# Layer 0 of a four-layer scan network as one sequence of scans

## The chip, the core and the metric

The kernel runs on one core of a Trainium2 chip. The metric is the device time of one execution in microseconds (us). Engines are called PE (matrix), DVE (vector), ACT (scalar), POOL (GpSimd) and SP (which here issues all the transfers). Everything is computed in float32.

## The reference, cut to what matters

The network has four layers over images of 4 x 48 x 48 x 192. The change concerns layer 0, two "bimambas" with a norm and a residual between them:

```python
xw = jnp.swapaxes(x, 1, 2).reshape(Bb, Ww * Hh, C)
xw = _bimamba(xw, 0, P)                      # pair 0
xh = jnp.swapaxes(xw.reshape(Bb, Ww, Hh, C), 1, 2).reshape(Bb, Hh * Ww, C)
xh = _ln(xh, norm_w, norm_b) + x.reshape(Bb, -1, C)   # the "mix"
xh = _bimamba(xh, 2, P)                      # pair 2
# _bimamba(u, i, P) = _mamba(u, P[i]) + _mamba(u[:, ::-1], P[i + 1])
```

A `_mamba` projects 192 channels to 2 x 384 (inner part and gate z), runs a causal convolution of three taps and a silu over the sequence, projects to dt, B and C, and makes for each of 384 channels and 16 states the recurrence

```python
h = exp(delta * A) * h + (delta * u) * b      # over the 2304 tokens
y = sum over the 16 states of h * c
```

then adds D * u, multiplies by silu(z) and projects back to 192. The second sequence order is the image by rows where the first was by columns, so the mix has to turn each image.

## The kernel before, in words

**A job** (`MambaJob`, L496) is 384 tokens of one image in one direction; six make a pass. Layer 0 has for each pair four images x two passes x six jobs = 48 jobs. The backward pass of an image adds the forward pass's result (`prior`) to its own, and stores it mirrored. **A group** is 128 channels x 4 states x 384 tokens; a job has 3 x 4 = 12, and its groups are called slots 0 to 11 here. One group does:

- ACT makes the four decays `a` (`decay`, L365), two groups ahead;
- DVE multiplies `du` by the broadcast B rows `bcb` into `inputs`, and scans (`scan`, L401);
- POOL copies the scan's last column into `state`, multiplies `h` in place by the C rows (`weigh`, L419), and writes the entering state of the next group but one into its `bcb` (`carry`, L382, the copy `bcb<-state`);
- PE sums the four states of `h` into `y` by identity matmuls (`reduce`, L433), one group behind; a float32 matmul is two instructions.

`h` goes round a ring of four buffers (`hs`), `bcb` one of five in layer 0 and in layer 3 (`bcs`), where a job fetches four, each 1540 KB broadcast from DRAM.

**The order** is written out by hand in `run_jobs` (L738). PE, DVE, POOL and ACT work in the order of the program; only SP's transfers are placed by the scheduler. Besides the group's own steps each slot has the *units* of the next job (`units`, L548: projections, convolution, dt, gate, each a PE part and an ACT part) and the *outputs* of the previous one (L625). A backward job's outputs end with two adds of `prior` on POOL, in slots 7 and 8. So a job's preparation runs while the job before it scans. POOL also has `drive` (slots 1, 5, 9) and `gate` (slots 2, 6, 10), each one product of 128 x 384.

`mamba_pair` (L899) loads the weights of a pair, opens the pools and runs its 48 jobs. It is called twice (L1616 to L1623). Between, `mix_images` (L926) runs by itself: it loads the sums of all images, normalizes them in stages on PE, DVE and ACT (`norm_stages`), turns them and adds the residual on DVE and POOL (L956), writes `mixed`, and loads pair 2's weights, whose diagonal matrices DVE makes (L859, L866).

Layers 1 and 2 already have **side steps**: a `Side` (L692) holds lists of small steps, and each slot may begin one whose kind (`pe`, `act`, `pool`, `both`, `dma`) is allowed in that slot. `Normed` (L1146) makes the steps of a layer norm. Layer 0 doesn't use them.

Of the kernel before, what the change touches and what calls it, by code (L numbers as in the profile page):

```python
# [17 lines left out]
B = 4  # L18
# [204 lines left out]
class ScanPools:  # L223
# [6 lines left out]
    def __init__(self, k, ctx, parts, rows):  # L230
        pool = k.tc.tile_pool
        self.parts, self.rows = parts, rows
        self.wide = 128 // parts
        self.n = N // parts
        self.groups = self.n // NG
        self.W = W = CH if rows else CH + 1
        self.one = ctx.enter_context(pool(name="one", bufs=1))
        self.two = ctx.enter_context(pool(name="two", bufs=2))
        self.bcs = ctx.enter_context(pool(name="bcs", bufs=5 if parts == 1 else 4))
        self.hs = ctx.enter_context(pool(name="hs", bufs=4))  # L240
        self.y = ctx.enter_context(pool(name="y", bufs=2 if rows else 1, space=PSUM))
        self.ps = ctx.enter_context(pool(name="ps", bufs=2, space=PSUM))
        self.vec = ctx.enter_context(pool(name="vec", bufs=1, space=PSUM))

        inputs = k.tile(self.vec, [128, 1536 if rows else 2048], "inputs")
        self.b = inputs[:, : NG * W].rearrange("p (j l) -> p j l", l=W)
        self.du = k.tile(self.vec, [128, 512], "du")[:, :W]
        self.ones = k.tile(self.one, [128, 1], "ones")
        k.nc.vector.memset(self.ones, 1.0)
        self.decays = [k.tile(self.one, [128, NG, W], f"a{i}") for i in range(3)]  # L250
        self.n_decays = 0
        self.revs = [None] * 3
        self.yts = 3 if rows else 2
        self.rev = None

        self.sum = k.ident
        if parts == 2:
            self.sum = k.tile(self.one, [128, 64], "sum")
            k.nc.vector.tensor_tensor(self.sum, k.ident[:, :64], k.ident[:, 64:], ALU.add)
# [28 lines left out]
class ScanJob:  # L288
# [6 lines left out]
    extras = ()  # L295

# [199 lines left out]
class MambaJob(ScanJob):  # L496
# [5 lines left out]
    skips = True  # L502
# [45 lines left out]
    def units(self, last):  # L548
# [41 lines left out]
        if self.twin is not None:  # L590
            self.z = self.twin.z
            outputs = last.outputs((7, 7), (9, 9), (10, 10), (11, 11)) if last is not None else []
            bc, deltas = self.projections(lambda: self.xs, (3, 3), (5, 5))
            return [conv(0, 0, 0), conv(1, 1, 2), conv(2, 2, 2), bc, *deltas, *outputs]
        outputs = last.outputs((4, 4), (6, 6), (7, 7), (8, 8)) if last is not None else []
# [29 lines left out]
    def outputs(self, *slots):  # L625
# [10 lines left out]
        def add(m):  # L636
            k.g.tensor_tensor(self.o[:, m, :], self.o[:, m, :], prior[:, m, :], ALU.add)
            if m == 1:
                store()
# [24 lines left out]
        if self.prior is not None:  # L664
            prior = k.tile(self.pools.one, [Q, 2, CH], "prior")
            k.nc.sync.dma_start(prior, halves(self.prior)[:, :, d0 : d0 + CH])
            units += [(slots[2 + m], lambda: None, lambda m=m: add(m)) for m in range(2)]
# [24 lines left out]
class Side:  # L692
# [4 lines left out]
    slots = {"pe": (0, 4, 5), "both": (0, 4), "act": (0, 4, 5), "pool": (0, 2, 4, 5), "dma": range(6)}  # L697

    def __init__(self, k, psum):
        self.k, self.psum = k, psum  # L700
        self.waiting, self.rest = [], None
# [36 lines left out]
def run_jobs(jobs, side=None):  # L738
# [29 lines left out]
    for t in range(len(groups) + gated):  # L768
# [8 lines left out]
        if at == taken + 3 and n + 1 == len(jobs) and n:  # L777
            Stream(jobs[n - 1].outputs(*[(0, 0)] * 4)).run(per)
# [20 lines left out]
        if side is not None and t < len(groups):  # L799
            if at == taken + 1 and n:  # L800
# [10 lines left out]
    Stream(jobs[-1].outputs(*[(0, 0)] * 4)).run(per)  # L811
# [37 lines left out]
class MambaWeights(Weights):  # L849
    def __init__(self, k, pool, inT, xpT, dtT, vec, tag):  # L850
        super().__init__(k, pool, 128, 12, xpT, dtT, vec, tag)
        self.decays(k)
        nc = k.nc
        self.k, self.pool, self.in_src = k, pool, inT
        self.D = self.vec[:, :, 17:18]
        self.cb = self.vec[:, :, 18:19]
        self.diagD = k.tile(pool, [128, 3, 128], f"diagD{tag}")
        for i in range(3):
            nc.vector.tensor_scalar(  # L859
                self.diagD[:, i, :], k.ident, self.D[:, i, :], None, ALU.mult  # L860
            )
        self.taps = vec.shape[1] - 19
        self.diag = k.tile(pool, [128, 3, self.taps, 128], f"diag{tag}")
        for i in range(3):
            for t in range(self.taps):
                nc.vector.tensor_scalar(  # L866
                    self.diag[:, i, t, :],
                    k.ident,
                    self.vec[:, i, 19 + t : 20 + t],
                    None,  # L870
                    ALU.mult,
                )

    def enter(self, tag="inT"):

        self.inT = self.k.tile(self.pool, [Q, 2, 768], tag)
        self.k.nc.sync.dma_start(self.inT, self.in_src.rearrange("(k p) m -> p k m", p=Q))

# [20 lines left out]
def mamba_pair(k, weights, srcs, first, outs, ahead=None):  # L899


    with ExitStack() as ctx:
        pool = ctx.enter_context(k.tc.tile_pool(name="w", bufs=1))
        ws = []

        def load():
            for n, (inT, xpT, dtT, vec, outT) in enumerate(weights):
                w = MambaWeights(k, pool, inT, xpT, dtT, vec, f"_{n}")
                w.enter(f"inT_{n}")
                w.outT = k.tile(pool, [128, 3, C], f"outT_{n}")  # L910
                k.nc.sync.dma_start(w.outT, outT.rearrange("(k p) m -> p k m", p=128))
                ws.append(w)

        if ahead is None:
            load()
        else:
            ahead(load)
        pools = ScanPools(k, ctx, 1, False)
        jobs = []
        for b in range(B):  # L920
            jobs += mamba_pass(k, pools, ws[0], False, srcs[b], first[b])
            jobs += mamba_pass(k, pools, ws[1], True, srcs[b], outs[b], True, first[b])
        run_jobs(jobs)


def mix_images(k, o, hw, norm, out_hw, load):  # L926

    nc, tc = k.nc, k.tc
    with (
        tc.tile_pool(name="mx", bufs=2) as pool,  # L930
        tc.tile_pool(name="mx1", bufs=1) as one,
        tc.tile_pool(name="mxp", bufs=6, space=PSUM) as psum,
    ):
        nw = k.tile(one, [Q, 2, 2], "nw")
        s0, s1, res = {}, {}, {}

        def fetch(b):
            s0[b] = k.tile(pool, [Q, 2, L], "s0")
            for n in range(2 if b == 0 else 1):
                at = slice(0, L) if b else (slice(0, CH), slice(CH, L))[n]  # L940
                nc.sync.dma_start(s0[b][:, :, at], halves(o[b])[:, :, at])
                if b == 0 and n == 0:
                    nc.sync.dma_start(nw, norm.rearrange("(k p) v -> p k v", p=Q))
            s1[b] = k.tile(pool, [Q, 2, L], "s1")
            res[b] = k.tile(pool, [Q, 2, L], "res")
            nc.sync.dma_start(res[b], halves(hw[b]))

        def pre(b):
            if b + 1 < B:
                fetch(b + 1)  # L950
            if b == 1:
                load()

        def post(b):
            for m in range(2):
                (nc.vector, nc.gpsimd)[m].tensor_tensor(  # L956
                    square(res[b][:, m, :]),
                    square(res[b][:, m, :]),
                    flipped(s1[b][:, m, :]),
                    ALU.add,  # L960
                )
                nc.sync.dma_start(out_hw[b][m * Q : (m + 1) * Q, :], res[b][:, m, :])

        def chunk(img):
            return lambda b, c: img[b][:, :, c * CH : (c + 1) * CH]

        stages = norm_stages(
            k, pool, psum, chunk(s0), chunk(s1), k.mean192, 1e-5, nw[:, :, 0], nw[:, :, 1]
        )
        fetch(0)  # L970
        pipelined(stages, pre, post)
# [174 lines left out]
class Normed:  # L1146
# [22 lines left out]

    def image(self, c, src, steps, dst):  # L1170

        def move(out, in_):
            return lambda: self.k.nc.sync.dma_start(out, in_)

        def parts(out, in_):
            n = L // 3
            at = [slice(i * n, (i + 1) * n) for i in range(3)]
            return [[("dma", move(out[:, :, a], in_[:, :, a])) for a in at]]  # L1180

        ahead = parts(self.turned, src) if c == NCH - 1 else []
        return [*ahead, steps, *(parts(dst, self.turned) if c == 0 else [])]
# [25 lines left out]
    def norm(self, srcs, eps, g, bias, out, tag="nx", last="act"):  # L1209
# [22 lines left out]
        def root(ps):  # L1232
            rs = st["rs"] = self.tile([Q, CH], "nrs")
            k.act(rs, ps, AF.Ln, bias=self.eps[:, eps : eps + 1])
            k.act(rs, rs, AF.Exp, scale=-0.5)
            scale(0)
# [5 lines left out]
        def affine(dst, m):  # L1242
# [7 lines left out]
            ("both", (Q, lambda: [(k.mean192, st["sq"][:, m, :]) for m in range(2)], root)),  # L1250
            ("pool", lambda: scale(1)),
# [38 lines left out]
def scan_layers(k, pool, layers, ends, ahead):  # L1290
# [4 lines left out]
    with ExitStack() as ctx:  # L1295
# [5 lines left out]
        side = Side(k, pools.ps)  # L1301
# [166 lines left out]
class RowWeights:  # L1468
# [4 lines left out]
    def __init__(self, k, pool, raw, psum, sets):  # L1473
        self.pairs = []
        for s, (ws, _) in enumerate(sets):
            w = MambaWeights(k, pool, *ws[:4], f"_{s}")
            self.pairs.append((w, copy(w)))
# [122 lines left out]
def network(tc, d, out):  # L1600
    with ExitStack() as ctx:
# [8 lines left out]
        def pair(first):  # L1610
# [5 lines left out]
        hw, wh = ([d[n][b] for b in range(B)] for n in ("x_hw", "x_wh"))  # L1616
        first, o = images("first"), images("oa")
        mamba_pair(k, pair(0), wh, first, o)
        mixed, x1 = images("mixed"), images("x1")
        mamba_pair(  # L1620
            k, pair(2), mixed, first, x1,
            lambda load: mix_images(k, o, hw, d["L0_norm"], mixed, load),
        )  # L1623
# [90 lines left out]
def layout(i):  # L1714
    x = np.moveaxis(i["x"], -1, 1)
    d = {"x_hw": x.reshape(B, C, L), "x_wh": swapped(x).reshape(B, C, L)}
# [82 lines left out]
```

## Time and profile before

| | us |
|---|---|
| median of 3 runs (19842.79 to 19854.58) | 19849.5 |
| the profiled execution | 19853.7 |
| its span | 19851.9 |
| DVE busy | 18186.9 (92%) |
| PE busy | 17508.4 (88%) |
| POOL busy | 14713.3 (74%) |
| ACT busy | 12793.6 (64%) |
| mean granted PE clock | 0.939 |

Layer 0's first pair scans from 44.8 us to 3136.5 us, its second from 3335.4 to 6426.5; then come the inputs of layer 1, the scans of layers 1 and 2, of layer 3, and the last part. The rows of the timeline read: start, duration, engine, line (often a helper's: L56 is the wrapper of DVE, POOL and PE, L93 that of ACT), operation, output<-inputs, shape, and in brackets the engine's idle time before it with what ended it. A busy PE is not PE at its peak, since matmuls overlap.

### The profile page before, as it was taken

How to read it: one execution, taken by the hardware profiler on the slowest of the kernel's cores; microseconds unless marked ns; L12 is line 12 of the kernel's file. 1: busy time of each engine (PE TensorE's matmuls, PEld its weight loads, DVE VectorE, ACT ScalarE, POOL GpSimd, SP SyncE). 2: the span in 40 equal slices, each digit the busy share in tenths (PEclk: the TensorE clock that was granted, in tenths of full speed). 3: DMA queues.
4: the chain of work that ended last, by engine and by line, in shares of the span. 5: the costliest groups of instructions: out<-in, count | busy, mean ns of one | idle time of the engine just before them, and what ended most of it. 6: DMA issues, size and time to landing. Idle time of an engine off the chain costs nothing. (4 is left out here: it accounts for less than half of the span.)

```text
span 19851.9 us, 159333 instructions
## 1 busy us (share of the span) xinstructions
PE 17508.4 (88%) x48144; PEld 8277.2 (42%) x48144; DVE 18186.9 (92%) x7432; ACT 12793.6 (64%) x22445; POOL 14713.3 (74%) x10864
## 2 busy tenths in 40 slices
PE   8999997999998878888888888889999989999989
PEld 4444443444444422333333333334444444444444
DVE  8999997999999599999999999969999999999993
ACT  6666665666666466666666766766666666666663
POOL 7887875888787177888888888857777777777770
PEclk9999998999999989999999999989999999999999
DMA  3333333333333366666666666642233233332331
GB/s 116 107 110 114 108 107 120 106 109 115 112 107 106 79 134 139 146 145 148 143 145 146 138 145 144 139 115 104 104 107 106 99 108 109 107 106 103 108 107 46
DMA packets 495754, 2313.41 MB, mean 117 GB/s; under 512 B 76360, under 2 KB 329584, under 8 KB 340336
## 3 DMA queue, kind: packets, MB, share of 16 engines
q1 hardware_dynamic: 494896, 2303.22, 41.3%
q8 instruction: 386, 6.32, 0.1%
q14 instruction: 472, 3.87, 0.1%
HBM read 2110.68 MB, written 192.32 MB: 116 GB/s over the span
## 5 line engine op out<-in xcount | busy, mean ns | idle before, releaser
L56 POOL TENSOR_TENSOR h<-h,bcb 128x1536 f32<-128x1536 f32 x3456 | 11909.0, 3446 | 1712.8 <-DVE h L56 1437.2
L56 DVE TENSOR_TENSOR_SCAN h<-a,inputs 128x1540 f32<-128x1540 f32 (+1 forms) x3456 | 11609.1, 3359 | 449.8 <-ACT a L93 12.0
L93 ACT ACTIVATE a<-delta,A 128x384 f32<-128x384 f32 (+1 forms) x13824 | 7432.7, 602 | 3325.5 <-DVE h L56 3312.8
L56 PE MATMUL y<-h,ident 128*128 128x384 f32 x18432 | 6788.0, 517 | 562.8 <-POOL h L56 557.9
L56 DVE TENSOR_TENSOR inputs<-du,bcb 128x1540 f32<-128x1540 f32 (+1 forms) x3456 | 6115.1, 1769 | 471.1 <-ACT du L93 105.3
L56 PEld LDWEIGHTS y<-h,ident 128*128 128x128 f32 x18432 | 3621.6, 201 | 3586.6 <-POOL h L56 1068.4
L56 PE MATMUL y<-h,sum 128*64 128x384 f32 x9216 | 3664.9, 547 | 599.1 <-POOL h L56 471.2
L56 PEld LDWEIGHTS y<-h,sum 128*64 128x64 f32 x9216 | 1290.9, 150 | 2917.1 <-issue 1752.9
L56 POOL COPY state<-h 128x4 f32<-128x4 f32 x2304 | 431.6, 187 | 2243.8 <-DVE h L56 2228.9
L56 PE MATMUL ps<-xh,diag 128*128 128x384 f32 x4032 | 1418.2, 491 | 197.2 <-ACT xc L93 197.2
L56 PE MATMUL ps<-u,inT 96*128 96x384 f32 x3456 | 1268.3, 499 | 217.0 <-ACT z L93 135.0
L56 PE MATMUL ps<-bcd,dtT 12*128 12x384 f32 (+1 forms) x2304 | 1018.2, 550 | 384.4 <-ACT delta L93 381.0
L56 PEld LDWEIGHTS ps<-xh,diag 128*128 128x128 f32 x4032 | 751.3, 189 | 790.1 <-ACT xc L93 284.7
L93 ACT ACT_TABLE_LOAD x794 | 1018.7, 1283 | 14.1
L90 ACT ACT_TABLE_LOAD x787 | 1009.7, 1283 | 14.2 <-PEq L1789 0.7
L56 PEld LDWEIGHTS ps<-u,inT 96*128 96x128 f32 x3456 | 655.3, 193 | 734.8 <-ACT z L93 214.4
L93 ACT ACTIVATE delta<-ps,vec 128x384 f32<-128x384 f32 x1152 | 631.0, 578 | 300.1 <-PE ps L56 293.1
L56 PE MATMUL ps<-yt,outT 128*96 128x384 f32 x2304 | 789.8, 486 | 0.7 <-POOL yt L56 0.7
L56 PEld LDWEIGHTS ps<-bcd,dtT 12*128 12x128 f32 (+1 forms) x2304 | 383.3, 192 | 954.5 <-ACT delta L93 618.3
L93 ACT ACTIVATE du<-dus 128x384 f32<-128x384 f32 x1152 | 558.3, 485 | 165.6 <-DVE inputs L56 158.2
L56 POOL TENSOR_TENSOR dus<-delta,xc 128x384 f32<-128x384 f32 x576 | 574.7, 998 | 75.9 <-ACT delta L93 75.9
L93 ACT ACTIVATE o<-ps 96x384 f32<-96x384 f32 x288 | 140.0, 486 | 720.5 <-PE ps L56 720.5
(131 smaller groups left out, 9679.2 us busy)
## 6 DMA issues: line engine op xcount, KB each, us to landing
bcb<-bc SPq DMA_DIRECT2D x384, 1540.0 KB
bcb<-bc SPq DMA_DIRECT2D x768, 770.0 KB
bcb<-bc SPq DMA_DIRECT2D x384, 1536.0 KB
y<-o SPq DMA_DIRECT2D x192, 288.0 KB
xs<-xi_wh SPq DMA_DIRECT2D x96, 288.0 KB
xs<-xi_hw SPq DMA_DIRECT2D x96, 288.0 KB
added<-y SPq DMA_DIRECT2D x96, 288.0 KB
xs<-x_wh SPq DMA_DIRECT2D x96, 288.0 KB
```

Of the source, the lines that this page charges most:

```text
L56: return lambda *a, **kw: self.tc.keep_in_program_order(op(*a, **kw))
L90: self.in_order(self.nc.scalar.preload_act_table_set(LOG_EXP))
L93: return self.in_order(self.nc.scalar.activation(out, in_, func, **kw))
```

## The change

Layer 0 becomes one `run_jobs` over 96 jobs (`layer0`). The mix of an image is made as side steps of the backward jobs of pair 0: when the job after it reaches slot 9, a job offers its list, of which each allowed slot takes one: centre the first half (PE, ACT; slot 9), the second half (slot 11), and in the next job the variance with its root (slot 1), the scale of both halves in one POOL instruction (slot 3), the load of the residual into the square's buffer (slot 4), the affine on ACT (slot 5) and two POOL adds that write the sum in row order into `turned`, one image in SBUF (slot 7). After an image's last job three transfers write it to `mixed` (slots 8, 0, 4). The residual is now taken in column order, so the input in row order is no longer passed.

The weights of pair 2 are loaded into the tiles of pair 0, in extra steps of two jobs (the forward weights in the second backward job of the last image, the backward ones in the second job of pair 2); their decays and diagonals are made on ACT. The rings get smaller in layer 0: `bcb` from five to four, `h` from four to three. The two adds of `prior` become one of both halves, in layer 0 in slot 8 and in layer 3 in slot 11. The norm's root is written over the squares in all layers.

```diff
-        self.bcs = ctx.enter_context(pool(name="bcs", bufs=5 if parts == 1 else 4))
-        self.hs = ctx.enter_context(pool(name="hs", bufs=4))
+        self.bcs = ctx.enter_context(pool(name="bcs", bufs=5 if rows else 4))
+        self.hs = ctx.enter_context(pool(name="hs", bufs=4 if rows or parts == 2 else 3))
...
-            outputs = last.outputs((7, 7), (9, 9), (10, 10), (11, 11)) if last is not None else []
+            outputs = last.outputs((7, 7), (9, 9), (11, 11)) if last is not None else []
...
-        outputs = last.outputs((4, 4), (6, 6), (7, 7), (8, 8)) if last is not None else []
+        outputs = last.outputs((4, 4), (6, 6), (8, 8)) if last is not None else []
...
-        def add(m):
-            k.g.tensor_tensor(self.o[:, m, :], self.o[:, m, :], prior[:, m, :], ALU.add)
-            if m == 1:
-                store()
+        def add():
+            k.g.tensor_tensor(self.o, self.o, prior, ALU.add)
+            store()
...
-            units += [(slots[2 + m], lambda: None, lambda m=m: add(m)) for m in range(2)]
+            units.append((slots[2], lambda: None, add))
...
-            if at == taken + 1 and n:
+            if n and at == jobs[n - 1].offered:
                 offer(jobs[n - 1])
...
+class PairWeights(MambaWeights):
...
+    def decays(self, k):
+        if not self.late:
+            return super().decays(k)
+        k.act(self.A, self.vec[:, :, 1 : 1 + N], AF.Exp)
+        k.act(self.A, self.A, AF.Copy, scale=-1.0)
+
+    def scaled(self, out, by):
+        if not self.late:
+            return super().scaled(out, by)
+        self.k.act(out, self.k.ident, AF.Identity, scale=by)
+
+    def extras(self):
+        return [
+            (0, self.load),
+            (8, lambda: self.decays(self.k)),
+            *((slot, lambda i=i: self.diagonals(i)) for i, slot in enumerate((8, 9, 11))),
+        ]
...
-def mamba_pair(k, weights, srcs, first, outs, ahead=None):
+def layer0(k, pairs, wh, norm, outs):
...
+        pools = ScanPools(k, ctx, 1, False)
+        slots = {"pe": (1, 9, 11), "pool": (3, 7), "act": (5,), "dma": (0, 4, 8)}
+        side = Side(k, pools.ps, slots)
...
+            def load(sq):
+                st["res"] = sq
+                nc.sync.dma_start(sq, halves(wh[b])[:, :, at : at + CH])
+
+            def add():
+                for m in range(2):
+                    k.g.tensor_tensor(
+                        rows_of(normed.turned[:, m, :], c),
+                        *(square_rows(st[v][:, m, :]) for v in ("x", "res")),
+                        ALU.add,
+                    )
+
+            steps = normed.norm(
+                lambda: [job.o], 0, nw[:, :, 0], nw[:, :, 1], affine, spare=load
+            )
+            steps.append(("pool", add))
+            return [steps, *(normed.parts(halves(mixed[b]), normed.turned) if c == NCH - 1 else [])]
...
+                some = mamba_pass(k, pools, there, False, src, first)
+                some += mamba_pass(k, pools, back, True, src, out, True, first)
+                if m == 0:
+                    for job in some[NCH:]:
+                        job.steps = lambda b=b, job=job: mix(b, job)
...
+        n = len(jobs) // 2
+        for i in range(2):
+            jobs[n + i * NCH - NCH + 1].extras = ws[1][i].extras()
+        run_jobs(jobs, side)
...
-def mix_images(k, o, hw, norm, out_hw, load):
...
+        def scale_both():
+            rs = st["rs"].unsqueeze(1).to_broadcast([Q, 2, CH])
+            k.g.tensor_tensor(st["x"], st["x"], rs, ALU.mult)
```

## The prediction

> **What bounds the kernel now.** I read the busy table and its forty slices first, then the stretches around the dip in slice 7, then the timeline of that dip, then that of one steady group of layer 0.
>
> ```profile
> DVE  8999997999999599999999999969999999999993
> ...
> L56 POOL TENSOR_TENSOR h<-h,bcb 128x1536 f32<-128x1536 f32 x3456 | 11909.0, 3446 | 1712.8 <-DVE h L56 1437.2
> L56 DVE TENSOR_TENSOR_SCAN h<-a,inputs 128x1540 f32<-128x1540 f32 (+1 forms) x3456 | 11609.1, 3359 | 449.8 <-ACT a L93 12.0
> ```
>
> VectorE (DVE) is the bound: 92% busy over the span; in layer 0 (slices 1 to 13) it dips at the start and in slice 7. The stretches (us; busy and count of PE, PEld, DVE, ACT, POOL; clock; DMA share; GB/s):
>
> ```profile
> 1700.00:3100.00 1400.00, 1276.60 (x3625) 668.54 (x3624) 1339.05 (x523) 930.82 (x1621) 1125.25 (x947) 0.97 0.32 110
> 3138.00:3335.00 197.00, 117.11 (x278) 54.32 (x276) 101.11 (x128) 74.42 (x124) 44.47 (x15) 0.73 0.55 142
> ```
>
> Inside the scans DVE has 1339 of 1400 us and POOL 1125. A group costs DVE 1.77 (inputs) + 3.36 (scan) and starts every 5.37 us (mean of the 575 differences between scan starts of the first pair); the other 0.24 is hand-over. Between the pairs stands the mix. The timeline of DVE there:
>
> ```profile
> 3133.09 3.36 DVE L56 TENSOR_TENSOR_SCAN h<-a,inputs 128x1540 f32<-128x1540 f32 x1
> ...
> 3303.19 0.06 DVE L249 MEMSET ones<- 128x1 f32 x1 [14.12 <-DMA mixed<-res]
> 3331.95 1.77 DVE L56 TENSOR_TENSOR inputs<-du,bcb 128x1540 f32<-128x1540 f32 x1 [28.70 <-ACT du L93]
> 3335.44 3.36 DVE L56 TENSOR_TENSOR_SCAN h<-a,inputs 128x1540 f32<-128x1540 f32 x1 [1.73 <-ACT a L93]
> ```
>
> The last scan of pair one starts at 3133.09 and the first of pair two at 3335.44: drain, norm, residual, turn, weights, and a fresh prologue, with no scan. One steady group on POOL, with the DVE rows that wait for it:
>
> ```profile
> 600.82 3.45 POOL L56 TENSOR_TENSOR h<-h,bcb 128x1536 f32<-128x1536 f32 x1
> 604.23 1.00 POOL L56 TENSOR_TENSOR o<-o,prior 96x384 f32<-96x384 f32 x1
> 605.17 0.19 POOL L56 COPY bcb<-state 128x4 f32<-128x4 f32 x1
> 605.92 0.19 POOL L56 COPY state<-h 128x4 f32<-128x4 f32 x1 [0.56 <-DVE h L56]
> ...
> 605.96 1.77 DVE L56 TENSOR_TENSOR inputs<-du,bcb 128x1540 f32<-128x1540 f32 x1
> ```
>
> This is slot 7 of a backward job. The `bcb<-state` copy (`carry`) must end before DVE's next inputs. With 1.00 us of extra POOL work it ends at 605.36, 0.60 before DVE starts; the hand-over takes about 0.1. So a slot hides about 1.5 us of extra POOL work, and each microsecond beyond stalls DVE.
>
> **The sum.** It is made on the profiled execution: 19853.7 us (span 19851.9, 1.8 around it), 4.2 above the median 19849.5.
>
> *The gap goes.* 3335.44 - 3133.09 - 5.37 (an ordinary step) = 197.0. Also in the last job of a pair DVE idles 3.26 us at 3104.35 for a carry queued behind two adds that wait for ACT and PE; in one sequence pair one has no such job: 3.2. Together **-200.2**. Nothing of the prologue stays: the job loop makes a job's units one job (64.4 us) before its scans, across the old border too.
>
> *POOL's side steps.* 24 jobs (backward passes of pair one) get a scale of 96x768 in slot 3 and two adds of 96x384 in slot 7; the residual add of two 998 ns halves in slots 7 and 8 becomes one 96x768 add in slot 8. No row has 96x768 on POOL; a line through 998 ns at 384 and 3446 at 1536 gives 1.81 us (at most 2.0, two halves). Slot 3: 1.81 - 1.5 = 0.3 late. Slot 7: two adds, 2.0 if the strided write costs nothing: 0.55 late. Slot 8: 1.81, begun on a POOL still 0.35 behind DVE: 0.35. Slots 9 and 10 carry 1.0 as before and slot 11 none, so it recovers. 1.2 us x 24 = **+28.8**. Bounds: nothing if POOL catches up unseen (a gain is excluded, as nothing is taken from those slots but the 2 x 1.0 counted); above, the dearest POOL row, the mix's 96x2304 add beside VectorE (10.40 us median, 4.5 ns an element): 3.46 in slots 3 and 7 and 2.0, 2.0 and 0.5 late, 4.5 x 24 = 108. I take the low side: 998 ns adds between SBUF tiles run beside these very scans 144 times, that mix row does not.
>
> *The merged add elsewhere.* 24 backward jobs of pair two: slot 8 alone, 0.3 x 24 = **+7.2** (bounds 0 and 0.5 x 24 = 12). Layer 3's scans over rows have no carry; slots 10 and 11 (gate + add, add) become gate, one add: 0.
>
> *PE and the ring of h, 4 to 3.* A scan may now start only when the matmuls on the h of three groups earlier have ended. I paired these in the trace for the 1,148 groups of layer 0: the least lead is 0.55 us, 25 are under 2, the median is 4.7; slots 2, 4, 6 are lowest (medians 3.1, 3.8, 2.4), slots 0, 1, 8, 10, 11 have 5.5 to 6. One case, from the timelines of PE and DVE:
>
> ```profile
> 578.52 2.20 PE L56 MATMUL ps<-xh,diag 128*128 128x384 f32 x6 [1.61 <-ACT xc L93]
> 580.56 2.75 PE L56 MATMUL y<-h,ident 128*128 128x384 f32 x8
> ...
> 586.39 3.36 DVE L56 TENSOR_TENSOR_SCAN h<-a,inputs 128x1540 f32<-128x1540 f32 x1
> ```
>
> The h of slot 2 (scan at 570.29) is read by PE until 583.31, the scan that would take its buffer starts at 586.39. The side's matmuls, 4 instructions (1.3 us at 0.33 each) in slots 1, 9, 11, fall on the long leads, and PE idles 1.6 for ACT in slot 3 before the short ones. I take **0**; below it nothing (a smaller ring frees nothing); above, the lead of slot 6 gone in all 96 jobs by 0.6 us: 58.
>
> *bcb ring, 5 to 4, and SP.* A job's first fetch now waits for the weighing of slot 8, as the other three already do (second fetch issued at 609.66, weighing ends 609.64). From there to its carry is 11.6 us; from issue to its last packet it takes 5.7 to 8.3 (median by position; 16.7 only in the prologues). On SP the new residual load (288 KB) stands behind `u` and ahead of the `bc` store, and waits for slot 3's scale, over before slot 5; the three stores of an image follow the last add. Cost 0; above, 1 us in each of 96 jobs, 96.
>
> *ACT.* Per side job two copies (0.49), two squares (0.48), Ln 0.58, Exp 0.52, two affines (0.70): 4.4 us of some 21 idle; Ln/Exp stand beside the decays, so no table load. ACT waits for DVE 3312.8 us in all, DVE for `a` 12.0. Cost 0 while the decays keep their two groups of lead; each microsecond over that is one of DVE.
>
> *Reload in place.* Two times seven loads (about 1 MB) spread over SP behind their last readers, and 12 small ACT scalings, in two jobs: **+2**, one late fetch (0 to 10). *Ends:* one more load on SP before the first `u` +0.5; the last job's add in one piece, +0.9 there and +0.8 in the tail: **+2.2**.
>
> 19853.7 - 200.2 + 28.8 + 7.2 + 2.0 + 2.2 = 19693.7; less the 4.2 to the median: **19690 us**.
>
> **A rule beside a row.** ScalarE's strided copies cost 0.85 against 0.49 us, so stride has a price here on one engine; POOL's has no row. The Trainium skill, GPSIMD Engine Reference, section "Performance pitfalls for Q7 kernels", puts reads stepped by over 8 bytes at half as much again; these adds step 192 bytes, but in the write. If writes paid likewise, slot 7 would hold an estimated 2.8 us and the sum grow by 19. The same page, section "Engine selection", speaks against the change: an elementwise add belongs on VectorE. The rows answer it: on DVE, scale (0.95) and adds (4.12 / 6 each, 1.37) would add 2.3 us to the bound per chunk; on POOL they cost my 1.2.
>
> **Rivals.**
> *POOL slow in strides or by contention.* For it: the mix's 10.4 us. Against: the 998 ns rows. It gives 19690 + 108 - 29 = 19770, still faster.
> *Late fetches.* For: four buffers fill each 5.37 us with 5.7 us transfers and side loads between. Against: 3.3 us of lead left. 19690 + 96 = 19786.
> *The ring of three h stalls the scan: the slower one.* PE ends later by the side's work or half-clock stretches. It begins to bite at 2.4 us later (slot 6), and eats the whole gain when a job loses (200 - 40) / 96 = 1.7 us. At 4.5 later slot 6 loses 2.1 and slots 2 and 9 about 0.9 more: 3 x 96 = 288, 19980. Halfway it ends level. Against: the leads above already hold the half-clock stretches.
> *The gap doesn't close:* the new weights or `mixed` are late at the border. The loads stand five jobs ahead; should the prologue's 28.7 us come back, 19720.
>
> **Chances.** Forecast (19655 to 19745, the unclosed gap in it) 0.72; POOL slow 0.12; late fetches 0.03; ring level 0.05; ring slower 0.07; something unseen and slower 0.01. A change of under 0.2% (40 us) can't be told from none here. Faster 0.87, same 0.05, slower 0.08. The range, 19655 (no POOL cost) to 19790 (dear POOL or late fetches), leaves out about 0.13.
>
> **What would show it.** No row of the mix, scan starts 5.37 apart across the border; in pair one's backward jobs inputs late after slots 3, 7, 8 with POOL `bcb` as releaser, about 0.3, 0.55, 0.35; in pair two only slot 8. Wrong if `DVE h` waits for PE (ring), POOL's carry for a DMA (fetch), or the turned adds take far over 1 us.

## The result and the profile after

The changed kernel takes 19717.0 us (median; 19711.9 to 19720.3), the kernel before beside it 19846.2 us (19839.1 to 19854.6). The ratio is 0.9935, 95% interval 0.9917 to 0.9952: 129 us faster. The forecast was 19690 us, range 19655 to 19790. The range held the time and the sign was right, but behind the 27 us between forecast and time stand terms that were wrong in opposite directions, one of them by 48 us.

The busy table's slices of the kernel after, and the two costliest groups:

```profile
DVE  8999999999998699999999999969999999999993
...
L56 POOL TENSOR_TENSOR h<-h,bcb 128x1536 f32<-128x1536 f32 x3456 | 11907.7, 3446 | 1704.9 <-DVE h L56 1429.9
L56 DVE TENSOR_TENSOR_SCAN h<-a,inputs 128x1540 f32<-128x1540 f32 (+1 forms) x3456 | 11606.6, 3358 | 440.6 <-ACT a L93 4.1
```

The 5 in slice 7, the gap between the pairs, is gone. The stretches that the prediction showed, of the kernel after (us; busy and count of PE, PEld, DVE, ACT, POOL; clock; DMA share; GB/s):

```profile
1700.00:3100.00 1400.00, 1302.29 (x3703) 690.00 (x3702) 1314.90 (x514) 962.14 (x1695) 1135.80 (x950) 0.96 0.33 112
3138.00:3335.00 197.00, 186.94 (x532) 99.79 (x531) 183.92 (x72) 142.18 (x259) 165.42 (x133) 0.95 0.36 122
```

The second row is what was wanted: DVE is busy 183.9 of the 197 us where it had been busy 101. The first row is what was not: inside the scans of pair one DVE fell from 1339 to 1315 busy us of the same 1400. The border between the pairs, DVE's timeline after:

```profile
3188.49 3.36 DVE L56 TENSOR_TENSOR_SCAN h<-a,inputs 128x1540 f32<-128x1540 f32 x1
3193.16 1.77 DVE L56 TENSOR_TENSOR inputs<-du,bcb 128x1540 f32<-128x1540 f32 x1 [1.31 <-ACT du L93]
3195.03 3.36 DVE L56 TENSOR_TENSOR_SCAN h<-a,inputs 128x1540 f32<-128x1540 f32 x1
```

The last scan of pair one and the first of pair two are 6.5 us apart instead of 202.3. The span by stretches, from the scan starts of four traces (two of them, the run with late centring and the last version, are experiments below):

| stretch, us | before | after | late centring | last version |
|---|---|---|---|---|
| to the first scan | 44.8 | 42.7 | 43.8 | 42.6 |
| pair one, first to last scan | 3088.3 | 3145.8 | 3101.4 | 3095.3 |
| the border | 202.3 | 6.5 | 5.3 | 5.3 |
| pair two, first to last scan | 3087.7 | 3095.4 | 3094.9 | 3089.1 |
| from there to the end | 13428.8 | 13424.3 | 13428.2 | 13423.0 |

So 195.8 us went at the border and 57.5 came back inside pair one. To see where, I took the 24 jobs that hold a merged add of pair one and a first centring (each the job after a backward one; the last is the first job of pair two) and every step between two scan starts in them, less the ordinary 5.37 us, and added up by slot ("step 8" runs from the scan of slot 8 to the scan of slot 9; step 11 leads to the next job):

| us in 24 jobs | step 4 | 8 | 9 | 10 | 11 | pair two, step 9 |
|---|---|---|---|---|---|---|
| before | 0.1 | -0.3 | 0.1 | -0.3 | 198.5 (the gap) | -0.2 |
| after | 3.5 | 5.9 | 3.5 | 1.2 | **49.1** | 4.4 |

Steps 4, 8 and 9 are those that the prediction named: the scale in slot 3, the turned adds in slot 7, the merged add in slot 8, each making POOL's carry late for the next slot but one. Step 11 it did not name. One job's end in the timeline of the kernel after, all engines:

```profile
604.54 1.97 POOL L56 TENSOR_TENSOR turned<-nx,nsq 96x384 f32<-96x384 f32 x2
606.45 0.19 POOL L56 COPY bcb<-state 128x4 f32<-128x4 f32 x1
606.67 1.77 DVE L56 TENSOR_TENSOR inputs<-du,bcb 128x1540 f32<-128x1540 f32 x1 [0.50 <-POOL bcb L56]
...
610.26 1.79 POOL L56 TENSOR_TENSOR o<-o,prior 96x768 f32<-96x768 f32 x1
612.11 2.31 PE L56 MATMUL ps<-o,center 96*96 96x384 f32 x4 [2.53 <-POOL o L56]
...
618.40 2.74 PE L56 MATMUL ps<-u,inT 96*128 96x384 f32 x8
...
621.18 0.49 ACT L93 ACTIVATE z<-ps 128x384 f32<-128x384 f32 x1 [0.80 <-PE ps L56]
...
624.52 0.47 ACT L93 ACTIVATE du<-dus 128x384 f32<-128x384 f32 x1
625.08 1.77 DVE L56 TENSOR_TENSOR inputs<-du,bcb 128x1540 f32<-128x1540 f32 x1 [2.22 <-ACT du L93]
```

The first three rows are the known cost: the copy `bcb<-state` ends at 606.64 and DVE has lost 0.50 us. Then the new one. The first centring of the norm stands in slot 9 on PE; it reads `o`, which POOL's merged add finishes at 612.05 only. PE stood still for 2.53 us, and behind the centring, in PE's order, stand the reductions and the gate's projections of the next job (`ps<-u,inT`, done at 621.14). The last gate's silu starts 0.04 us after them, then come ACT's second table load, three decays and `du`, for which DVE waits 2.22 us. The kernel after, waits (us in total, times, longest):

```profile
DVE inputs L56 <- ACT du L93: 96.4, 41, 26.0
...
DVE inputs L56 <- POOL bcb L56: 54.4, 124, 2.4
...
PE ps L56 <- POOL o L56: 53.2, 24, 3.3
```

The kernel before has the first kind of wait fewer times, and 88.6 us of it in three fresh prologues: 27.4 at the start, 28.7 between the pairs, and the longest, 32.5, at the start of layer 3:

```profile
DVE inputs L56 <- ACT du L93: 105.3, 19, 32.5
```

The theory taken from this (A): the 48 us are the first centring's wait for the merged add, passed on by in-order queues. Rivals: (B) ACT's 4.4 us of added work per side job is by itself too much before the next job; (C) the ring of three `h` buffers.

### The profile page after: what moved, and what is told of

It reads as the page before. It is cut to its first block, busy times and chain, and to the rows that moved or that the text cites. A ratio compares the mean times of both kernels' runs of the same rounds, so it can differ in the third digit from the quotient of the medians.

```text
span 19714.8 us, 159611 instructions
## 1 busy us (share of the span) xinstructions
PE 17500.7 (89%) x48240; PEld 8295.6 (42%) x48240; DVE 18084.7 (92%) x7310; ACT 12837.2 (65%) x22569; POOL 14746.4 (75%) x10860
## 4 chain that ended last, share of the span: by engine, by line
DVE 39%; POOL 33%; PE 13%; issue 10%; ACT 3%; DMA 2%; DVEq 0%; SPq 0%; POOLq 0%; ACTq 0%
POOL h L56 25%; DVE h L56 25%; DVE inputs L56 13%; PE y L56 5%; PE ps L56 4%; POOL dus L56 3%; PE vps L114 2%; POOL state L56 1%; ACT a L93 1%; DMA bcb<-bc 1%; POOL yt L56 1%; POOL bcb L56 1%; PE mop L114 1%; PE mps L114 1%; ACT L93 1%
## 5 line engine op out<-in xcount | busy, mean ns | idle before, releaser
L56 DVE TENSOR_TENSOR inputs<-du,bcb 128x1540 f32<-128x1540 f32 (+1 forms) x3456 | 6114.4, 1769 | 503.7 <-ACT du L93 96.4
```

Source lines behind the costliest of these rows:

```text
L56: return lambda *a, **kw: self.tc.keep_in_program_order(op(*a, **kw))
```

## The experiments

**1. The producer a slot earlier.** The merged add and the turned adds change places.

```diff
-        outputs = last.outputs((4, 4), (6, 6), (8, 8)) if last is not None else []
+        outputs = last.outputs((4, 4), (6, 6), (7, 7)) if last is not None else []
-        slots = {"pe": (1, 9, 11), "pool": (3, 7), ...
+        slots = {"pe": (1, 9, 11), "pool": (3, 8), ...
```

> The changed kernel with two POOL steps exchanged: the add of prior in slot 7, the two turned adds in slot 8. Theory A (the first centring matmul of slot 9 waits for POOL's add of prior, ACT waits for that matmul, and DVE in the next slot 0 waits for ACT's du): in slot 9 the sum is ready when PE comes to it, the 2.0 us that DVE loses between slot 11 and slot 0 in 24 jobs fall to the 0.07 of the kernel before, POOL's own lateness (0.5 a job in slots 4, 8, 9) stays: 19717 - 46 = 19671. Theory B (ACT's added work alone, 0.97 us of copy and square ahead of the gates and du, makes du late): nothing changes, 19717 within 5. Theory C (the ring of three h): nothing changes, 19717.

Measured: 19686.4 us, ratio 0.9919 (0.9904 to 0.9933). Step 11 fell from 49.1 to 4.1 us, the others stayed (4.4 in step 8, 5.1 in step 9): 45 of the 48 us hung on that wait. ACT's work and the ring are those of the change, and for B and C nothing was to change: neither is the main cause. The time is 15 us over what A expected, of which 8 lie in the scans of layer 3, which no edit touches (last section).

**2. The consumer two slots later.** Centring in slots 11 and 0 instead of 9 and 11, all POOL work as in the change.

```diff
-        slots = {"pe": (1, 9, 11), "pool": (3, 7), ...
+        slots = {"pe": (0, 1, 11), "pool": (3, 7), ...
```

> The changed kernel with the centring moved from slots 9 and 11 to 11 and the next slot 0 (variance in slot 1 as before); the add of prior stays in slot 8. Theory A: the add is long over, and ACT meets the copies behind du: 19717 - 46 = 19671, slots 11 to 0 back to 5.44. Theory B: ACT's copies no longer stand ahead of du: the same 19671. Theory C (ring of h): 1.3 us of PE moved from slot 9 into slot 0 make the matmuls on h later there: no gain, or slower than 19717.

Measured: 19673.2 us, ratio 0.9912 (0.9895 to 0.9928). Steps 4, 8, 9 read 3.5, 6.0, 3.6 as after; step 11 reads 1.2. The ring is three deep here too, so C falls as the cause of the 48 us. The same job's end, timeline of the run with late centring:

```profile
609.34 1.80 POOL L56 TENSOR_TENSOR o<-o,prior 96x768 f32<-96x768 f32 x1
...
611.80 1.16 PEld L56 LDWEIGHTS ps<-u,inT 96*128 96x128 f32 x4
612.12 1.45 PE L56 MATMUL ps<-u,inT 96*128 96x384 f32 x4
...
620.04 0.47 ACT L93 ACTIVATE du<-dus 128x384 f32<-128x384 f32 x1
```

The add ends at 611.14, but nothing on PE waits for it. From its end to `du` it is 8.9 us, after the change 12.5; `DVE inputs` waits for `ACT du` 17 times and 45.0 us, against 41 times and 96.4 after. The 24 that went are the 24 side jobs.

**3. The producer a slot later: a larger dose.**

```diff
-        outputs = last.outputs((4, 4), (6, 6), (8, 8)) if last is not None else []
+        outputs = last.outputs((4, 4), (6, 6), (9, 9)) if last is not None else []
```

> The changed kernel with the add of prior one slot later, in slot 9, so that the centring matmul of slot 9 waits about one group (5.4 us) longer. Theory A: the loss between slots 11 and 0 grows from 2.0 to about 7 in 24 jobs, +120, and slot 9 holds 2.8 us of POOL work in 48 jobs, some 1.1 late where slot 8 was 0.3 late, +40: about 19870. Theory B: only the POOL part, 19757. Theory C: 19757.

Measured: 19892.2 us in one execution, slower than the kernel before and 22 us over A's figure: one slot decides over the whole gain. Steps 10 and 11 read 132.3 and 71.6 us. Of its waits:

```profile
PE ps L56 <- POOL o L56: 182.3, 24, 8.7
...
DVE h L56 <- PE y L56: 94.5, 23, 6.7
```

PE's wait grew from 53 to 182 us as A says. The second row is rival C after all, as a consequence: with PE this late the scan itself waits until PE has read the buffer of `h` that it wants. The ring of three did not cause the stall of the change, but it has little left for a late PE. Not all of the loss is the centring's: pair two, which has none, lost some 20 us too: 22.8 in its step 10, where the add stands beside POOL's other work of slot 9 and the carry comes late, less the 4.4 of its step 9.

**4. No side steps.** Pair two reads the sums of pair one directly; the norm, the turn and the residual are not computed.

```diff
-                    for job in some[NCH:]:
-                        job.steps = lambda b=b, job=job: mix(b, job)
+                    mixed[b] = out
```

> The changed kernel without the mix: no side steps at all (no norm, no turn, no residual), pair 2 reads the sum of pair 1 as it stands. It leaves out part of the computation. It prices the side steps in one piece and tests the gap: if the whole gap of 200 us goes and the side steps cost what the 24 jobs show (47 by du, 13 by POOL), 19717 - 60 = 19657. If the rings of three h and four bcb cost anything by themselves, it stays above that by as much; up to 58 (h) or 96 (bcb) were my bounds.

Measured: 19664.6 us in one execution. Steps 4, 8 and 11 read -0.3, -0.3 and 1.2; step 9 keeps 4.7 for the merged add. This is what the closed gap is worth with nothing put into the groups; the late centring comes within 9 us of it.

**5. The shallower rings alone**, in the kernel before (`hs` 3 and `bcs` 4 in layer 0).

```diff
-        self.bcs = ctx.enter_context(pool(name="bcs", bufs=5 if parts == 1 else 4))
-        self.hs = ctx.enter_context(pool(name="hs", bufs=4))
+        self.bcs = ctx.enter_context(pool(name="bcs", bufs=5 if rows else 4))
+        self.hs = ctx.enter_context(pool(name="hs", bufs=4 if rows or parts == 2 else 3))
```

> The kernel before with the change's shallower rings in layer 0 alone (three buffers of h in place of four, four of the fetched B and C in place of five). The forecast's term: nothing, so 19845 within 6 us, and layer 0's slots keep their 5.37 us. Rival, the ring of h as the limit (the upper end of the forecast's term was 58 us): 19870 to 19905, as stalls before the matmuls that read h. Rival, late fetches (upper end 96 us): 19880 to 19940, as stalls of the input multiplication on the fetched tile.

Measured: 19854.5 against 19847.7 us, ratio 1.0004 (0.9995 to 1.0013), no difference. No step of layer 0 changed by over 2.1 us in its 24 jobs apart from the gap's, and pair one and pair two took 3088.1 and 3087.8 us. The forecast's zero for both rings holds for a PE that is on time.

**6. The merged add alone**, in the kernel before, in layers 0 and 3.

```diff
-        def add(m):
-            k.g.tensor_tensor(self.o[:, m, :], self.o[:, m, :], prior[:, m, :], ALU.add)
-            if m == 1:
-                store()
+        def add():
+            k.g.tensor_tensor(self.o, self.o, prior, ALU.add)
+            store()
```

> The kernel before with the two half-width adds of the forward sum merged into one full-width add on GpSimd, in layer 0's two pairs, and nothing else of the change. Theory A (the add hurts only through the centring matmul that waits for it, besides a GpSimd lateness of 0.2 to 0.3 us for each of 48 adds): 48 x 0.2 to 0.3 = 10 to 14 us, so 19855 to 19859, all of it in slot 9, with slot 11 as before. Rival, the longer add itself delays ScalarE's chain and so the next job's first input multiplication by 2 us a job: 48 x 2 = 96 more, 19950. Rival, hidden: 19845.

Measured: 19867.7 against 19847.7 us, ratio 1.0009 (1.0000 to 1.0019). Step 9 reads 4.7 us in pair one and 4.4 in pair two (0.19 a job), step 11 is that of before: without a centring behind it the longer add stalls nothing but the next carry. That is 9 of the 20 us; of the other 11, 6 stand in the scans of layers 1 and 2, which this edit does not touch, and they are not explained.

**7. Which queue passes the wait on?** ACT's copy out of the centring also stood idle, 5.70 us, so either queue could be the carrier. First, every step's second part was written one slot later than its first.

```diff
+        if side is not None and side.late:
+            side.end()
         stream.run(at if at < per - 1 else per)
...
             side.slot(at)
-            side.end()
+            if not side.late:
+                side.end()
```

> The changed kernel with ScalarE's part of each side step written one slot later than its matmuls: the matmuls of the first centring stay in slot 9 behind the merged add, but ScalarE's copy out of them stands behind the next slot's decays. It tells apart by which queue the wait reaches the next job's du. If it is ScalarE's queue alone (the copy that waits holds decays, silus and du): the 47 us go, 19670 to 19676. If it is TensorE's queue alone (the gate's matmuls stand behind the centring): they stay, 19712 to 19720. If both queues carry a share: between, about 19690.

Measured: 19770.5 us, ratio 0.9962 (0.9947 to 0.9977). This run could not decide: the edit put POOL's steps a slot later too, so the turned adds stood right before the merged add and steps 9 and 10 lost 35.2 and 12.9 us. So a second one deferred the matmul steps alone:

```diff
-            if not side.late:
+            if not side.late or not side.matmul:
                 side.end()
```

> The changed kernel with ScalarE's part of a side step written one slot later than its matmuls, for the steps that have matmuls alone; all GpSimd steps keep their slots, unlike in the run that deferred every step. If the wait reaches the next job's du through TensorE's queue (add, centring, the reductions behind it, the gate's projections, the gate, du): the slot 11 stall stays at 45 to 50 us and the time at 19710 to 19722. If through ScalarE's queue alone: slot 11 below 5 us and 19670 to 19678.

Measured: 19713.8 us, ratio 0.9929 (0.9913 to 0.9946). The stall stayed, though smaller, 34.7 us in step 11. The same job's end in the timelines of ACT and PE:

```profile
612.62 2.13 ACT L93 ACTIVATE a<-delta,A 128x384 f32<-128x384 f32 x4 [3.25 <-DVE h L56]
612.69 1.93 PE L56 MATMUL ps<-o,center 96*96 96x384 f32 x4 [3.32 <-POOL o L56]
614.72 0.49 ACT L93 ACTIVATE nx<-ps 96x384 f32<-96x384 f32 x1
...
618.98 2.74 PE L56 MATMUL ps<-u,inT 96*128 96x384 f32 x8
...
621.76 0.49 ACT L93 ACTIVATE z<-ps 128x384 f32<-128x384 f32 x1 [0.80 <-PE ps L56]
...
625.10 0.47 ACT L93 ACTIVATE du<-dus 128x384 f32<-128x384 f32 x1
```

ACT now makes its decays before the copy, and the copy no longer waits. But PE's centring still does, and `du` comes at 625.10. From the add's end to `du` the median of the jobs is 12.46 us in both kernels, and in each of the 24 jobs, in both, the gate's last silu starts 0.03 to 0.04 us after the end of the last projection. So PE's queue is the main carrier. The stall is smaller because the projections end 7.4 us after the add in 11 of the 24 jobs, where 9.1 is usual. What differs there is the pace of PE behind the wait. PE's timeline in the job above, then in the next one, in which the wait was shorter:

```profile
612.69 1.93 PE L56 MATMUL ps<-o,center 96*96 96x384 f32 x4 [3.32 <-POOL o L56]
614.42 1.49 PE L56 MATMUL y<-xc,diagD 128*128 128x384 f32 x2
615.70 3.45 PE L56 MATMUL y<-h,ident 128*128 128x384 f32 x8
618.98 2.74 PE L56 MATMUL ps<-u,inT 96*128 96x384 f32 x8
...
679.97 1.53 PE L56 MATMUL ps<-o,center 96*96 96x384 f32 x4 [0.87 <-POOL o L56]
681.34 0.81 PE L56 MATMUL y<-xc,diagD 128*128 128x384 f32 x2
681.98 2.75 PE L56 MATMUL y<-h,ident 128*128 128x384 f32 x8
684.57 2.74 PE L56 MATMUL ps<-u,inT 96*128 96x384 f32 x8
```

From the start of the centring to the gate's projections the same 14 matmuls take 6.29 us in the one and 4.60 in the other: for a while they start 0.64 us apart instead of 0.32. The two stretches (us; busy and count of PE, PEld, DVE, ACT, POOL; clock; DMA share; GB/s) have granted clocks of 0.73 and 1.00:

```profile
612.60:619.00 6.40, 6.31 (x15) 3.47 (x16) 5.96 (x3) 4.74 (x8) 5.61 (x8) 0.73 1.04 337
679.90:686.30 6.40, 6.33 (x20) 3.72 (x21) 5.98 (x3) 4.89 (x9) 5.62 (x8) 1.00 0.98 321
```

The other jobs show the same. In the changed kernel the 17 jobs in which PE stood for 1.94 to 3.33 us before the centring take 6.29 us or more for these matmuls, and their step 11 is 2.44 us too long in the mean; the seven in which it stood for 0.87 to 1.00 us take 4.60, and step 11 is 1.08 too long. In this run 13 jobs are slow (waits of 2.03 to 3.33, step 11 2.24 too long) and 11 are not (0.51 too long); eight of these waited 0.87 to 1.01 us, but three 2.02 to 3.00, so the length of the wait alone does not decide. With no wait at all (the exchanged adds) all 24 take 4.5.

By the means of the two kinds of jobs the slower pace makes 13 x 1.73 = 22 of the 34.7 us here, and 17 x 1.36 = 23 of the 48 in the changed kernel: about half of the price, or more, is the lower clock behind the wait, the rest the standing itself. No run holds the clock up behind such a wait, so this split is read from the jobs and not tested by an edit. ACT's queue has a small share: in the seven jobs of the changed kernel that kept the pace, the gate's last projection waits for ACT's first silu (0.30 us in one), which stands behind the copy.

The Trainium skill ("PSUM — Partial Sum Buffer", section "Engine vs sequencer instructions") states that matmuls start and complete in program order, and that a weight load may overlap matmuls in flight. The rows agree: after the change PE stands still for 2.53 us and starts the reductions of that slot (`y<-h,ident`) only at 615.49, behind the centring; with late centring they start at 609.43, before the add has even ended.

**8. A version without the stall and with smaller pieces.** Matmuls in slots 0, 1, 2; scale in two halves (slots 3, 4); turned adds one by one (7, 11); ACT's step in slot 6; the add of `prior` in halves where a job has no side steps.

```diff
-        slots = {"pe": (1, 9, 11), "pool": (3, 7), "act": (5,), "dma": (0, 4, 8)}
+        slots = {"pe": (0, 1, 2), "pool": (3, 4, 7, 11), "act": (6,), "dma": (0, 5, 8)}
...
+            parts = (0, 1) if self.steps is None else (slice(None),)
```

> The changed kernel with the side's matmuls in slots 0, 1 and 2 of the next job, its scaling in halves in slots 3 and 4, its turned adds singly in slots 7 and 11, ScalarE's step in slot 6, and the add of the forward sum in halves where there are no side steps. Theory A and the sum by slots: the run with the late centring stood at 19673; of its layer 0, 3.5 us in slot 4 and 6.0 in slot 8 were the side's GpSimd pairs and 4.4 in slot 9 of pair two the merged add. With no GpSimd piece over 1.0 us but the merged adds of pair one, 12 to 14 us of these go: 19659 to 19664. Rival, matmuls in slots 0 to 2 collide with the input projections and the convolution there and delay the next decays: 19680 to 19700. Rival, the split pieces cost what the pairs did (each piece's fixed part): 19673.

Measured: 19670.2 us, ratio 0.9911 (0.9896 to 0.9925). Steps 4 and 11 and pair two's step 9 read -0.3, 1.2 and -0.2 as hoped, but step 8 rose to 12.6. One case in this run, DVE's timeline:

```profile
607.64 3.36 DVE L56 TENSOR_TENSOR_SCAN h<-a,inputs 128x1540 f32<-128x1540 f32 x1 [1.25 <-PE y L56]
```

ACT's step in slot 6 made `delta` late (it begins 0.7 us before the scan of slot 8 in this job, 2.2 us before it in experiment 9), PE's projections from it stood longer before the reductions, and the scan waited for the ring of `h` (9.9 us in all; 2.7 after the change) and partly for decays (11.7 us; 4.1 after).

**9. The same with ACT's step back in slot 5**, and for that the scale whole in slot 3.

```diff
-        slots = {"pe": (0, 1, 2), "pool": (3, 4, 7, 11), "act": (6,), "dma": (0, 5, 8)}
+        slots = {"pe": (0, 1, 2), "pool": (3, 7, 11), "act": (5,), "dma": (0, 4, 8)}
```

> The changed kernel with the side's matmuls in slots 0, 1 and 2, its scaling whole in slot 3, ScalarE's step back in slot 5, the turned adds singly in slots 7 and 11, and the add of the forward sum in halves where there are no side steps. Reason: in the version before this one the 12.6 us of slot 8 were scans that waited for decays, behind ScalarE's step moved to slot 6. Expected by slots of the side jobs: slot 4 3.5 us, slot 8 under 3, slot 9 under 5, slot 11 under 2, slot 9 of pair two 0, so 19660 to 19666. Rival, the matmuls in slots 0 to 2 are what makes the decays late: slot 8 stays at 12 us and the time at 19670.

Measured: 19661.7 us (19657.0 to 19663.8), ratio 0.9903 (0.9888 to 0.9917), the fastest of all. Steps 4, 8, 9, 11 read 3.5, -0.2, 4.5, 1.2, and pair two's step 9 -0.2, each as expected. The reason given there was half right: the waits were for the ring of `h` as much as for decays (they are 1.5 and 4.6 us now), but both hung on ACT's step. It stands 55 us under the changed kernel and level with the version that computes no mix at all; the two are not told apart, and that one still has pair two's merged adds whole (4.5 us).

## Why the prediction was right, and where not

*The gap.* Forecast -200.2; measured 202.3 to 6.5 at the border, and the stall of 3.2 in the last job of a pair gone. Right. The border's 6.5 holds 1.1 of the new stall. The rival of a gap that stays open did not happen: new weights and `mixed` were in time.

*POOL's side steps.* Forecast +28.8; measured 15.5: steps 4, 8 and 9 lost 12.9 against -0.1, and the forward jobs into which the last side steps of an image fall 2.5. Mechanism and places were right, the size was not, for two reasons. Where a job lost, it lost 0.24, 0.39 and 0.18 in steps 4, 8, 9, not 0.3, 0.55 and 0.35, so a slot hides a little more than the 1.5 us I gave it. And I multiplied by 24: the first job of a pass has no carry to be late, and lost nothing, so there are 20. The durations were right: 1.81 us forecast for the 96x768 product, 1.81 measured; 1.0 for a turned add, 1.01 measured. POOL slow in strides did not happen: the add that writes with a step of 192 bytes took 1010 ns, the contiguous ones 996. The Trainium skill's price for strided reads ("GPSIMD Engine Reference", "Performance pitfalls for Q7 kernels"), which the prediction weighed, is not to be carried over to these writes.

*The merged add elsewhere.* Forecast +7.2; measured 4.6 in pair two.

*PE and the ring, the fetch ring, SP, the reload.* All at or near nothing, and measured so: alone (experiment 5), and in the changed kernel, where no step apart from those named here lost more than a microsecond over its jobs. The exception is step 10 (1.2 against -0.3): in four jobs the scan of slot 11 waited for PE to read `h` (0.54 us in one), behind the centring's wait. The slower rival was right in mechanism and wrong in place: it needs a late PE, which the ring's lead in the trace of before could not show, and the half-clock stretches that it named did come, new ones, behind the centring.

*ACT, and the side's matmuls.* This is the step that failed: "Cost 0 while the decays keep their two groups of lead", and of PE that the side's matmuls "fall on the long leads". I costed what the side steps take of each engine, and asked of the ring whether PE's 1.3 us had room. I did not ask when their operand would be ready. I moved the add from slots 7 and 8 (halves that PE had no part in) to one piece in slot 8, and put the first reader of its result in slot 9 at the head of PE's queue, with the gate's projections, the gate and `du` behind it. The sum priced such a wait elsewhere (the carry queued behind two adds in the last job of a pair); the wait of PE for POOL was not seen as one. Its price was 48 us (49.1 less the 1.2 that stays with late centring), 2.0 us a job, and with it came what the sum had no term for either: PE's lower clock behind the wait, some half of the 48 (experiment 7). Rows of the trace of before would have told the wait:

```profile
606.19 3.45 POOL L56 TENSOR_TENSOR h<-h,bcb 128x1536 f32<-128x1536 f32 x1
...
607.01 1.46 PE L56 MATMUL ps<-u,inT 96*128 96x384 f32 x4
```

There POOL's product of slot 8 ends at 609.64, so a merged add behind it ends near 611.45, while the gate's first projection, after which the centring was to stand, ends on PE at 608.47. That is a wait of some 3 us on PE (2.53 in the job shown), in a queue with the next job's gate in it.

*The ends.* First scan forecast 0.5 later, measured 2.1 earlier. Behind layer 0, 4.5 us less where I had 0.8 more; the scans of layer 3 alone are 9 us shorter, most of it by the stalls of the last section.

The sum once more, against the profiled execution after (span 19714.8 and the 1.8 around it, 19716.6): the forecast's 19693.7 lacks 23 us, which are 48 for the stall and 1.5 for the ring behind it, less 13 for POOL's lateness, 3 for the merged add and some 11 for the reload and the ends. The closeness of the forecast owes something to these opposite errors, which is luck.

## What to carry to other kernels

When work is put into the slack of a tuned loop, its busy time on each engine is only half of its price: for every operand that comes from another engine, compare when it is ready with when the reading queue gets there, and charge the difference to whatever stands behind it in that queue, up to the first thing that the bounding engine needs. Here two more slots between producer and reader are worth 44 us, and the producer one slot later costs 175 (some 20 of them in pair two, which has no such reader), which eats the whole gain and more. Look also at the clock behind the wait: here PE ran some of the matmuls behind most waits of 2 to 3.3 us at half its pace, and that was about half of the price, or more. Where a side step produces on a loaded engine, place its reader late and cut the pieces to what one slot hides.

## What else the runs showed

In layer 3, 20 to 22 of the 1151 steps are 0.35 us long over the rest in four of the kernels (before, the exchanged adds, the rings, the merged add), some 8 us in all, and only one in each of the other eight. They lie 159 to 488 us apart, never closer. The run with exchanged adds has them and the changed kernel does not, though the exchange touches nothing in layer 3. One of them, DVE's timeline in the run with exchanged adds:

```profile
14175.16 1.77 DVE L56 TENSOR_TENSOR inputs<-du,bcb 128x1536 f32<-128x1536 f32 x1
14177.41 3.35 DVE L56 TENSOR_TENSOR_SCAN h<-a,inputs 128x1536 f32<-128x1536 f32 x1 [0.48 <-DVE inputs L56]
```

The scan begins 0.48 us after its own engine's last instruction, with nothing else late. So about 8 us of a difference between two builds of this kernel can come from a part that neither changed, which is as much as the last two versions were made for; what decides it stays open. The kernel before has them and the changed kernel does not, so some 8 of the change's 129 us are of this kind.
